# Splitting the next x within a step at the switch, and another order of stores and loads in the queue of a recurrent layer

## The chip, the cores and the metric

The kernel runs on one core of a Trainium2 chip. The metric is the time of the program on the device in microseconds (us), as the median of several runs. A profile comes from one further execution; its times are counted from the start of its span. The engines are named as the profile names them: PE (TensorE, the matrix unit; PEld are its weight loads), DVE (VectorE), ACT (ScalarE), POOL (GpSimd) and SP (SyncE, which issues nearly all DMA transfers of this kernel, in program order).

## The reference

x has 64 sequences of 256 steps with 1024 features, in float32. The first layer is a recurrence over the steps, added to its input:

```python
xW = jnp.einsum('ntd,dh->nth', x, Wx) + b
def step(prev_h, xw):
    next_h = jnp.tanh(prev_h @ Wh + xw)
    return (next_h, next_h)
x = x + h_of_all_steps
```

The second layer takes Haar differences and sums of its input over all levels, multiplies them by a gate of 1024 values per sequence (two small layers on the condition) and puts them together again. Since every part is multiplied by the same gate and the transform is undone, this is `v + v * gate`, and with the residual around it the result is `x * (2 + gate)`. The kernel calls `2 + gate` the `factor`.

## The kernel before, in words

All is computed in one pass over the steps t = 0 to 255. Two kinds of matrix products share PE.

*Products of h.* h (64 x 1024) times Wh is done by Strassen's seven products, in the order 1, 4, 2, 5, 6, 7, 3 (the calls of `strassen_product` in the loop over t, L1065 to L1104). Each is 32 small matmuls. `strassen_sides` forms the seven left sides from `hT`, the transposed h; side 4 is the quarter 3 of `hT` itself. The accumulators for the next step get their share of x @ Wx ahead of time by a copy on ACT (`put_part`, L632). Within a step DVE adds the products up (L1074, L1076, L1094, L1095, L1099, L1102, L1105), ACT takes the tanh (L1048) and DVE transposes the quarters (L1052). At the end of a step `residual` (L639 or L642) adds h to x on DVE.

*Products of x.* x of two steps (a "pair") is a 128 x 1024 tile. To reach float32 precision it is split in three: `x_high` by a mask (L138), `x2` by `difference` (L320), `x1` by `low` (L315) on DVE, and `x0` by `cast` (L326) on ACT. `beside_two` issues the products (L881): those with `x2` go to the banks `mixed`, those with `x1` and `x0` to the banks `main`. `both_mixed` takes the `mixed` banks out, and `finish(0)` and `finish(1)` (L802, on DVE) take the two `main` banks out. The products 5 and 7 of the next step of h write the same two banks. The finished sum of a pair goes to DRAM (`store_sum`, L789) and comes back in another layout as the shares of two steps: eight transfers (`reload_two`, L782), four for each step. POOL then adds the bias to each half (L785).

A *group* is one such set of products of x and the two steps of h that follow it. The last step of a group calls `beside_two` at its end, which issues the next group's work. From the 23rd step on (`SWITCH = 22`) a pair is one of three kinds. The first six are "plain". After that "one" and "two" alternate, 55 of each: the last two of the eight blocks of features of two pairs are done together by Strassen's method, for which weight forms are loaded again and again from DRAM (`load_slot`, L775), and in a "two" group POOL forms the sides for the following pair (L813 to L816), which DVE splits in the next step (L823, L826 and L831, by the lists `within` and `behind_residual`: what is in `within` runs in the first step of a group between the transpose of quarter 0 and L1094, what is in `behind_residual` after that step's `residual`).

*The switch.* Up to step 21 the results go out as pairs, from large tiles called slabs. From step 22 on each step's x is loaded by itself (`load_step`, L724, a tile `r` of 256 KB, three buffers), gets h added (L639), is multiplied by the factor on POOL (L861) and stored (`store_step`, L720). The slabs' space is given to new tiles at the end of step 21 (`start_of` is true in that call of `beside_two`), so that the first load of x after it waits for the last stores from slabs. In that call the x that is split is the pair 13.

*The order of the work.* It is written out by hand for all engines: each engine and SP's queue run their instructions in the order of the program. In `beside_two` a dictionary `at` says before which matmul of x the pieces of work on the other engines are placed, counted in matmuls; `per` is the number of matmuls to one bank. `not_ahead_of` makes `store_sum` wait for a copy in the last step of a group, so that transfers stay out of most of the products of h; what is behind it in SP's queue waits too.

Of the kernel before, what the change touches and what calls it, by code (L numbers as in the profile page):

```python
# [91 lines left out]
def tile_cond_resid(  # L92
# [193 lines left out]
    def bank(tag: str, name: str):  # L286
        return one_pool.tile([P, HALF], F32, tag=tag, name=name)
# [11 lines left out]
    class XWork:  # L299
# [12 lines left out]
        def low(self) -> None:  # L312
            i, x = self.i, pairs[self.i]
            self.x1 = split.tile([P, D], F32R, tag="x1", name=f"x1_{i}")
            nc.vector.tensor_sub(self.x1, x, self.high)  # L315

        def difference(self) -> None:
            i = self.i
            self.x2 = split.tile([P, D], F32R, tag="x2", name=f"x2_{i}")
            nc.vector.scalar_tensor_tensor(  # L320
                out=self.x2, in0=self.high, scalar=1.0 + DOWN, in1=pairs[i], op0=ALU.mult, op1=ALU.subtract
            )
# [63 lines left out]
        def finish(self) -> list:  # L386
            for h in range(2):
                self.finish_half(h)
            return self.relay()
# [84 lines left out]
    for k in range(B):  # L474
        x_block(k)
        split_block(k)
        if k == 0:
            now = XWork(1)
# [47 lines left out]
    for t in range(ALONE):  # L526
        i, s = divmod(t, S)
# [34 lines left out]
        if s == 1 and t + 1 < ALONE:  # L562
            now = later
# [62 lines left out]
    def quad(v, j: int):  # L626
        return v[:, j * E : (j + 1) * E]

    def put_part(t: int, j: int):

        part = bank(("acc", "m57", "gate")[j], f"acc{t}_{j}")[:, :E]
        nc.scalar.copy(part, xws[t // S][t % S][:, j])  # L632
        return part
# [78 lines left out]
    within, behind_residual, ready = [], [], {}  # L712
# [6 lines left out]
    def store_step(t: int) -> None:  # L719
        nc.sync.dma_start(out=yS[t - SWITCH], in_=steps.pop(t))  # L720

    def load_step(t: int):
        steps[t] = new["pool"].tile([P, W], F32, tag="r", bufs=3, name=f"r{t}")
        return nc.sync.dma_start(out=steps[t], in_=xS[t - SWITCH])  # L724
# [49 lines left out]
    def load_slot(p: int, j: int):  # L774
        return nc.sync.dma_start(out=weight(p, j).bitcast(F32), in_=forms_d[p][j])  # L775

    def reload_two(i: int, places: list, biased: bool) -> None:
        d = totals.pop(("d", i))[:].rearrange("(s g m) (q f) -> s q m g f", s=S, g=G, q=Q)
        xws[i] = places
        for s, v in enumerate(places):  # L780
            for q in range(Q):
                nc.sync.dma_start(out=v[q * R : (q + 1) * R].rearrange("m (g c) e -> m g (c e)", g=G), in_=d[s, q])  # L782
        for v in places if not biased else []:
            v = v[:].rearrange("p (g c) e -> p g (c e)", g=G)
            nc.gpsimd.tensor_add(v, v, new["b"][:].unsqueeze(1).broadcast_to((P, G, F)))  # L785
# [50 lines left out]

    def beside_two(t: int, now, mark):

        i = (t + 1) // S
        n = now.i  # L840
        start_of = t + 1 == SWITCH
        kind = "plain" if n < FIRST else "one" if n % 2 == 0 else "two"
        if start_of:
            totals[i] = later.sum
        store_sum(i, mark)
        places = [
            const.tile([P, 4, E], F32, tag="xw0", name=f"xw{t + 1}"),
            const.tile([P, 4, E], F32, tag="h0T", name=f"xw{t + 2}"),
        ]
        if start_of:  # L850
            reload_two(i, places, True)
# [14 lines left out]
        else:  # L866
            ends.append(new["pool"].tile([P, D], F32, tag="x", name="ends"))
            nc.sync.dma_start(out=ends[0][:, :W], in_=xN)
        load_step(t + 1)
        with_next = kind != "one" and n + 1 >= FIRST and n + 1 < NP  # L870
        if with_next:
            new["ahead"] = new["pool"].tile([P, 2 * P], F32, tag="ahead", name=f"ahead{n + 2}")
            nc.sync.dma_start(out=new["ahead"], in_=xT[n + 2][:, FULL * P :])
        if not start_of:
            reload_two(i, places, False)

        mixed, main = ([bank(f"{tag}{h}", f"{tag}{h}_{n}") for h in range(2)] for tag in ("mixed", "main"))
        x = (now.x0, now.x1, now.x2)
# [10 lines left out]
        nxt = [None]  # L889
# [25 lines left out]
        per = {"plain": B, "one": FULL + 1, "two": FULL}[kind]  # L915
# [58 lines left out]
        def finish(h: int) -> None:  # L974
            plus_main(left[:, cols(h)], main[h])

        at = {}
        if kind == "one":
            at = {
                7: [fifth],  # L980
                14: [mask],
                16: [first_two],
                25: [sixth],
                28: [low],
                34: [seventh],
                35: [lambda: finish(0), fourth_sum, third_sum],
            }
        else:
            at = {
                lead + 2 * per: [both_mixed, mask, difference],  # L990
                lead + 4 * per: [low],
                lead + 5 * per: [lambda: finish(0)],
            }
# [26 lines left out]
        while slots:  # L1020
            load_slot(*slots.pop(0))
        if not start_of:
            store_step(t - 1)
            store_step(t)
        load_step(t + 2)
        return nxt[0]

    jobs = [None]
# [4 lines left out]
    later, coming = beside_x(t, None, later, [t], None)  # L1033
    first = ALONE
    for t in range(ALONE, T):
        i, s = divmod(t, S)
        final = t == T - 1
        last_of_group = t == first + groups[0] - 1
        xw = xws[i][s]
        m16, m5, m7 = (bank(tag, f"{tag}_h{t}")[:, :E] for tag in ("m16", "main0", "main1"))  # L1040
        y = sums.tile([P, 4, E], F32, tag="y", name=f"y{t}")
        u = sums.tile([P, E], F32, tag="u", name=f"u{t}")
        h = work.tile([P, W], F32, tag="h", bufs=1, name=f"h{t}")
        hT = None if final else work.tile([P, W], F32, tag="hT", name=f"hT{t}")
        nxt = [None] * 3

        def tanh(j: int) -> None:
            nc.scalar.activation(quad(h, j), quad(h, j), AF.Tanh)  # L1048

        def transpose(j: int) -> None:  # L1050
            if not final:
                nc.vector.transpose(quad(hT, j), quad(h, j))  # L1052

        def put_next(j: int) -> None:
            if not last_of_group:
                nxt[j] = put_part(t + 1, j)

        def times_factor(v: slice) -> None:
            nc.vector.tensor_mul(h[:, v], h[:, v], ends[0][:, W + v.start : W + v.stop])

        def plus_x(v: slice) -> None:
            nc.vector.tensor_add(h[:, v], h[:, v], ends[0][:, v])
            nc.sync.dma_start(out=yT[i][:, W + v.start : W + v.stop], in_=h[:, v])

        strassen_product(m16, sides[1], 1, True)  # L1065
        nc.scalar.copy(y[:, 0], m16)
        if accs[1] is None:
            accs[1] = put_part(t, 1)
        if t == first and coming is not None:
            coming.cast()  # L1070
        strassen_product(accs[2], sides[4], 4)
        strassen_product(accs[0], sides[2], 2)
        strassen_product(m5, sides[5], 5, True)
        nc.vector.tensor_add(quad(h, 0), accs[0], y[:, 0])  # L1074
        tanh(0)
        nc.vector.tensor_add(y[:, 3], m5, xw[:, 3])  # L1076
        transpose(0)
        if final:
            times_factor(slice(0, E))
            plus_x(slice(0, E))  # L1080
        elif t > T - 4:

            v = steps[t - 1]
            nc.vector.tensor_mul(v, v, factor)
            store_step(t - 1)
        put_next(0)
        if t == first:
            while within:
                within.pop(0)()
        strassen_product(m16, sides[6], 6)  # L1090
        mark = nc.scalar.copy(u, m16)  # L1091
        if t >= SWITCH:
            loads_of(t, mark)
        nc.vector.tensor_add(y[:, 3], y[:, 3], u)  # L1094
        nc.vector.tensor_add(y[:, 2], accs[2], u)  # L1095
        put_next(2)
        strassen_product(m7, sides[7], 7, True)
        for o in (3, 2):
            nc.vector.tensor_add(quad(h, o), m7, y[:, o])  # L1099
        tanh(3)  # L1100
        tanh(2)
        nc.vector.tensor_add(y[:, 1], m5, u)  # L1102
        transpose(3)
        strassen_product(accs[1], sides[3], 3)  # L1104
        nc.vector.tensor_add(quad(h, 1), accs[1], y[:, 1])  # L1105
        tanh(1)
        if final:
            times_factor(slice(F, W))
            times_factor(slice(E, F))
            plus_x(slice(E, F))  # L1110
            plus_x(slice(F, W))
            break
        transpose(2)
        put_next(1)
        transpose(1)
        sides = strassen_sides(hT, t)
        accs = nxt
        if t == T - 2:
            residual(t, hT)
            nc.vector.tensor_mul(steps[t], steps[t], factor)  # L1120
            store_step(t)
        elif last_of_group:
            group = range(first, t + 1)
            first = t + 1
            del groups[0]
            if t + 1 < SWITCH:
                later, coming = beside_x(t, later, coming, list(group), mark)
            else:
                coming = beside_two(t, coming, mark)
        else:  # L1130
            residual(t, hT)
            while behind_residual:
                behind_residual.pop(0)()
# [38 lines left out]
```

## Time and profile before

| | |
|---|---|
| median of 3 runs | 3024.32 us (3021.7 to 3028.24) |
| the profiled execution | 3028.58 us |
| its span | 3026.7 us |
| PE busy in the span | 3007.1 us |
| DVE, POOL, ACT busy | 2204.1, 944.6, 915.9 us |
| mean granted clock of PE | 0.998 |
| transfers on SP's queue | 452.08 MB, 46.4% of the DMA engines' time |

A busy line gives an engine's time, its share of the span and its number of instructions. A line of waits reads: the engine and line that waited, the engine and line that ended the wait, the total in us, how many times, the longest. A line of the timeline gives start and duration in us, the engine, the line, the operation, its tiles and shapes, how many are merged, and in brackets the idle time before it with what ended it. A line of the window view gives the stretch, its length, the busy time of PE, PEld, DVE, ACT and POOL in it (instructions in parentheses), the clock granted to PE as a share of full speed, the busy share of the DMA engines and GB/s.

### The profile page before, as it was taken

Reading aid. Unit: us, or ns where it says so; the run is one execution under the profiler, and the core shown is the slowest. Engines: PE = TensorE matmul, PEld = TensorE weight load, DVE = VectorE, ACT = ScalarE, POOL = GpSimd, SP = SyncE. Lnnn points to the kernel's source line nnn. Section 1 sums busy time; section 2 is a strip of 40 time slices with the busy share of each in tenths; the row PEclk is TensorE's granted clock in tenths of the full one; section 3 lists DMA queues with packets and bytes.
Section 4 is the critical chain, followed back from the end, with each engine's and each line's share of the span. In section 5 each row is a group of like instructions: output and inputs, shape, how many; then the busy total and the mean of one; then the engine's idle time right before and its main releaser. Section 6 shows DMA issues by size and latency. Waiting matters only on the chain. (4 is left out here: it accounts for less than half of the span.)

```text
span 3026.7 us, 148299 instructions
## 1 busy us (share of the span) xinstructions
PE 3007.1 (99%) x63697; PEld 2680.0 (89%) x63697; DVE 2204.1 (73%) x5594; ACT 915.9 (30%) x2753; POOL 944.6 (31%) x800
## 2 busy tenths in 40 slices
PE   9999999999999999999999999999999999999998
PEld 6888888998898889988988988899889888898897
DVE  8555567777777777777777777777777777777776
ACT  3222222333333323223333332233332332332332
POOL 2233223332333332323323323333233333333322
PEclk9999999999999999999999999999999999999999
DMA  7334454445544544445445445444454454445543
GB/s 266 120 108 136 149 174 151 155 145 158 161 145 140 165 156 147 154 153 162 142 153 166 150 140 163 149 156 147 152 163 149 140 165 150 154 149 157 162 143 111
DMA packets 254196, 462.09 MB, mean 153 GB/s; under 512 B 35696, under 2 KB 109168, under 8 KB 253552
## 3 DMA queue, kind: packets, MB, share of 16 engines
q1 hardware_dynamic: 253408, 452.08, 46.4%
q8 instruction: 514, 8.42, 1.2%
q14 instruction: 130, 1.06, 0.1%
q10 hardware_dynamic: 144, 0.52, 0.1%
HBM read 313.00 MB, written 139.46 MB: 149 GB/s over the span
## 5 line engine op out<-in xcount | busy, mean ns | idle before, releaser
L881 PE MATMUL main<-wx,x 128*128 128x512 f32 x3052 | 746.4, 389 | 0.0
L861 POOL TENSOR_TENSOR r<-r,factor 128x512 f32<-128x512 f32 x230 | 317.9, 1382 | 1323.6 <-DVE r L639 1038.6
L881 PEld LDWEIGHTS main<-wx,x 128*128 128x128 f32 x3052 | 572.9, 188 | 119.1
L785 POOL TENSOR_TENSOR xw<-xw,b_h 128x512 f32<-128x512 f32 x230 | 363.2, 1591 | 345.9 <-DMA xw<-sum_d 318.5
L1048 ACT ACTIVATE h<-h 128x128 f32<-128x128 f32 x976 | 275.4, 306 | 524.7 <-DVE h L1074 314.3
L881 PE MATMUL mixed<-wx,x 128*128 128x512 f32 x1526 | 389.1, 399 | 0.0
L632 ACT COPY acc<-xw 128x128 f32<-128x128 f32 x726 | 186.1, 269 | 552.6 <-POOL xw L785 253.2
L881 PEld LDWEIGHTS mixed<-wx,x 128*128 128x128 f32 x1526 | 277.4, 188 | 76.6 <-issue 23.0
L1052 DVE STREAM_TRANSPOSE hT<-h 128x128 f32<-128x128 f32 x972 | 298.0, 307 | 39.9 <-ACT h L1048 38.2
L212 PE MATMUL acc<-wh,s 128*32 128x128 f32 x8160 | 273.6, 273 | 0.0
L212 PE MATMUL acc<-t,hT 128*32 128x128 f32 x8160 | 271.5, 273 | 1.1 <-DVE hT L1052 0.5
L212 PE MATMUL main_h<-t,s 128*32 128x128 f32 x7808 | 264.4, 273 | 7.8 <-DVE sum L802 5.8
L212 PE MATMUL acc<-wh,hT 128*32 128x128 f32 x8160 | 270.3, 273 | 0.0
L212 PE MATMUL m_h<-wh,hT 128*32 128x128 f32 x7808 | 262.0, 275 | 3.9 <-ACT u L1091 3.9
L212 PE MATMUL m_h<-t,s 128*32 128x128 f32 x7808 | 261.0, 273 | 0.0
L212 PE MATMUL main_h<-wh,s 128*32 128x128 f32 x7808 | 260.5, 273 | 0.0
L799 ACT ACTIVATE sum<-chain_mixed 128x512 f32<-128x512 f32 x220 | 131.6, 598 | 398.1 <-PE chain_mixed L881 398.1
L212 PEld LDWEIGHTS m_h<-wh,hT 128*32 128x32 f32 x7808 | 208.7, 110 | 46.9 <-issue 23.6
L212 PEld LDWEIGHTS acc<-wh,s 128*32 128x32 f32 x8160 | 231.2, 110 | 0.9 <-issue 0.9
L212 PEld LDWEIGHTS acc<-t,hT 128*32 128x32 f32 x8160 | 228.8, 110 | 2.8 <-issue 1.1
L212 PEld LDWEIGHTS main_h<-t,s 128*32 128x32 f32 x7808 | 221.4, 110 | 10.5 <-DVE sum L802 6.0
L212 PEld LDWEIGHTS acc<-wh,hT 128*32 128x32 f32 x8160 | 228.8, 110 | 0.1
(135 smaller groups left out, 4062.9 us busy)
## 6 DMA issues: line engine op xcount, KB each, us to landing
wx<-form SPq DMA_DIRECT2D x330, 256.0 KB, 3.0
x<-xT SPq DMA_DIRECT2D x128, 512.0 KB, 4.7
sum_d<-sum SPq DMA_DIRECT2D x127, 512.0 KB, 3.0
xw<-sum_d SPq DMA_DIRECT2D x1008, 64.0 KB, 3.2
r<-xS SPq DMA_DIRECT2D x233, 256.0 KB, 3.8
yS<-r SPq DMA_DIRECT2D x233, 256.0 KB, 4.1
ahead<-xT SPq DMA_DIRECT2D x55, 128.0 KB, 5.0
wh<-wh SPq DMA_DIRECT2D x8, 512.0 KB, 10.9
```

What stands on the lines that cost most here:

```text
L212: nc.tensor.matmul(out=out[q * R : (q + 1) * R], lhsT=a[:, k * R : (k + 1) * R], rhs=wh_s.sides[i][k][:, q], start=first and k == 0, stop= ...
L632: nc.scalar.copy(part, xws[t // S][t % S][:, j])
L785: nc.gpsimd.tensor_add(v, v, new["b"][:].unsqueeze(1).broadcast_to((P, G, F)))
L799: nc.scalar.activation(out, mixed, AF.Copy, scale=-1.0)
L861: nc.gpsimd.tensor_mul(steps[r], steps[r], factor)
L881: nc.tensor.matmul(out=out, lhsT=lhs, rhs=rhs, start=start, stop=stop, skip_group_check=True)
L1048: nc.scalar.activation(quad(h, j), quad(h, j), AF.Tanh)
L1052: nc.vector.transpose(quad(hT, j), quad(h, j))
```

## The change

It has two parts.

At the switch, mask, `difference`, `low` and `cast` of the next x are no longer placed beside the products of x in that call. `beside_two` returns the still empty list instead of the split x. Mask and `difference` are put into `within`, `low` and `cast` into `behind_residual`, so that they run in step 22. The next call takes the split x from the list.

In every call after that, and in part in that one, SP's queue has another order. The load of r for the first step of the next group moves from behind the load of x to the end, between the second y store and the other load of r. The first y store moves from behind the weight forms to the middle of the reloads of sums, behind the first four.

```diff
-    def reload_two(i: int, places: list, biased: bool) -> None:
+    def reload_two(i: int, places: list, biased: bool, between=None) -> None:
         for s, v in enumerate(places):
             for q in range(Q):
                 nc.sync.dma_start(out=v[q * R : (q + 1) * R].rearrange("m (g c) e -> m g (c e)", g=G), in_=d[s, q])
+            if s == 0 and between:
+                between()
...
     def beside_two(t: int, now, mark):
 
+        if isinstance(now, list):
+            now = now[0]
...
-        load_step(t + 1)
         with_next = kind != "one" and n + 1 >= FIRST and n + 1 < NP
...
         if not start_of:
-            reload_two(i, places, False)
+            reload_two(i, places, False, lambda: store_step(t - 1))
...
+        elif start_of:
+            at = {2 * per: [both_mixed], 5 * per: [lambda: finish(0)]}
         else:
             at = {
                 lead + 2 * per: [both_mixed, mask, difference],
...
         if not start_of:
-            store_step(t - 1)
             store_step(t)
+        load_step(t + 1)
         load_step(t + 2)
+        if start_of:
+            within.append(lambda: (mask(), difference()))
+            behind_residual.append(lambda: (low(), nxt[0].cast()))
+            return nxt
         return nxt[0]
...
-        if t == first and coming is not None:
+        if t == first and isinstance(coming, XWork):
             coming.cast()
```

## The prediction

> **What bounds the kernel now.** The page's first part says which engine fills the span:
>
> ```profile
> PE 3007.1 (99%) x63697; PEld 2680.0 (89%) x63697; DVE 2204.1 (73%) x5594; ACT 915.9 (30%) x2753; POOL 944.6 (31%) x800
> ```
>
> TensorE (PE) is busy for 3007.1 of 3026.7 us. Only what makes it wait can be won, so the waits of PE come next (us in total, times, longest):
>
> ```profile
> PE main_h L212 <- DVE sum L802: 5.8, 1, 5.8
> PE m_h L212 <- ACT u L1091: 3.9, 1, 3.9
> PE main_h L212 <- issue: 2.0, 4, 1.1
> ```
>
> The first is a single wait, for `finish` on VectorE. The second lies at 3002.9, in the last steps, which wait for the last reload. The window view gives the group of the first beside its neighbours:
>
> ```profile
> 275.08:298.55 23.47, 23.47 (x501) 21.11 (x497) 14.25 (x41) 6.92 (x23) 8.96 (x6) 1.00 0.45 138
> 298.55:329.94 31.39, 25.62 (x500) 22.68 (x496) 13.07 (x40) 6.79 (x22) 2.56 (x2) 0.89 0.38 139
> 329.94:353.41 23.47, 23.47 (x500) 21.10 (x496) 13.46 (x40) 6.76 (x22) 11.12 (x8) 1.00 0.37 116
> ```
>
> A group (x products, then two steps of h) takes 23.47 us with PE busy throughout; the group at the switch takes 31.39, so 7.92 us are lost there, the largest loss in the trace. The timeline of the switch tells why:
>
> ```profile
> 310.55 0.42 SPq L865 DMA_DIRECT2D x<-xT  x1
> 311.02 0.43 SPq L724 DMA_DIRECT2D r<-xS  x1
> ...
> 314.43 0.69 DVE L138 TENSOR_SCALAR x_high<-x 128x1024 int32<-128x1024 int32 x1 [13.26 <-DMA x<-xT]
> ...
> 315.23 1.23 DVE L320 SCALAR_TENSOR_TENSOR x<-x_high,x 128x1024 fp32r<-128x1024 f32 x1
> 316.37 1.22 DVE L315 TENSOR_TENSOR x<-x,x_high 128x1024 fp32r<-128x1024 f32 x1
> 317.50 1.28 DVE L802 SCALAR_TENSOR_TENSOR sum<-main,sum 128x512 f32<-128x512 f32 x2
> 318.24 1.94 PE L212 MATMUL main_h<-t,s 128*32 128x128 f32 x32 [5.77 <-DVE sum L802]
> ```
>
> VectorE sits 13.26 us at the mask (L138) for the next x, whose load SP could issue only at 310.55. The two `finish` (L802) are queued behind mask, difference and low. Product number 5 of step 22, the fourth in order, writes the bank that `finish(0)` reads, so PE waits from 312.47 to 318.24. Then PE runs at half clock for a while:
>
> ```profile
> 315.00:318.20 3.20, 0.00 (x0) 0.00 (x0) 3.10 (x5) 1.04 (x1) 0.00 (x0) 0.57 0.83 322
> 318.20:320.00 1.80, 1.76 (x36) 1.63 (x40) 0.78 (x2) 0.48 (x2) 0.00 (x0) 0.50 0.09 33
> 320.00:321.70 1.70, 1.70 (x40) 1.57 (x36) 0.51 (x2) 0.00 (x0) 0.00 (x0) 0.50 0.00 0
> 321.70:324.00 2.30, 2.30 (x80) 2.25 (x76) 1.39 (x6) 1.05 (x4) 0.00 (x0) 0.87 0.00 0
> ```
>
> So 5.77 us of the loss are the wait, and the other 2.15 mostly the slow clock after it (the blocks at 318.24 and 319.95 take 1.71 us start to start, against 0.87).
>
> **The change, part by part: the switch.** Mask, difference, low and cast leave the x window. `finish(0)` and `finish(1)` then wait for their products alone: as in the next group (339.41 and 341.23, with PE leaving the window at 341.05) they end at 308.7 and 310.5, before PE needs either bank (312.3). The wait of 5.77 and the slow clock go. What is late next: mask and difference now stand in step 22, between the transpose of quarter 0 and `y<-y,u` (L1094). I lay the next group's first step on the switch (its PE starts at 341.05, here 309.65: 31.40 earlier). The transpose would end at 313.98 and L1094 start at 345.99 - 31.40 = 314.59. The x load is issued as before, with nothing new ahead of it, so the mask starts at 314.43 again and L1094 at 316.37, the place that low has now: 1.78 late. Behind it on VectorE is the transpose of quarter 3, which step 23's second product in order (number 4, L1071) reads. In the pattern that transpose ends at 347.55 and the product starts at 348.06, a slack of 0.51. So PE stalls 1.78 - 0.51 = 1.27, say 1.3 us, at 316.66. The other transposes are 0.87 apart, like the products (0.87), and add nothing.
>
> Low and cast follow step 22's residual (about 319.6 to 320.3): low 1.2 us on VectorE, to 321.4, and cast 1.04 on ScalarE, about 318.4 to 319.5. Behind low waits step 23's first sum (L1074, due 319.95, so 1.5 late), behind cast the copy of m16, done by 319.8. What step 23's own products read was made in step 22; then come mixed products of x for 3.8 us, which need only the difference. They cover both; without that cover low's lateness would cost up to 1.5. The load of r for step 22 now stands behind top and low of Wx: low, issued at 311.97, takes 6.9 us to land (318.9), so r lands just before its use at 319.6; up to 3 us later would still be covered by the mixed products. POOL's order stays as it was.
>
> Bounds of the leftover stall: if x landed over 1.3 us sooner, 0; if it took the median of x loads, 4.7 us from issue instead of this one's 3.7, 2.3. I take 1.3, since the same load in the same queue was measured. Its clock: a stall of 1.07 us near 2999 kept 1.00:
>
> ```profile
> 2998.00:3000.00 2.00, 0.93 (x34) 0.66 (x23) 0.29 (x1) 0.31 (x1) 0.00 (x0) 1.00 0.05 16
> ```
>
> and the 5.77 us one lost it some 2.4 us in (0.57 as mean from 315.0), for about 6.8 us, that is 3.4 us of lost work if PE runs all along. 1.3 is nearest to 1.07, so I take 0 and keep 3.4 as the upper end. The Trainium skill, "TensorE: Matmul & The Clock Gate", Part 1, says that the clock halves after at least one idle window of about 3.4 us. By that rule no stall under 3.4 us costs clock and the sum is 3017.7 with no end above it; by the row, a drop after 2.4, it could be 3021.1, so the row decides.
>
> Switch: -7.92 + 1.3 = **-6.6 us**.
>
> **The queue, in 117 groups.** SP issues the same transfers: sum store, x, (ahead), four reloads, first y store, four reloads, (three forms), second y store, two r loads. The first r load moves back past 8 reloads, up to 3 forms and 2 stores: some 9 us later, issued near 1502.7 instead of 1493.4 in the group shown below, landing 3.8 later (median) at 1506.5; its reader (L639) runs at 1511.27, so 4.8 us of margin. After the other kind the margin is larger (issue 1523.6, reader at 1535.94). The first y store waits for a POOL product that ended at 1491.7, so it holds nothing up; it delays the second half of the reloads by its 0.43 us of issue. The second r load needed the first store landed:
>
> ```profile
> SPq L724 <- DMA yS<-r: 355.1, 116, 5.0
> ```
>
> This 3.1 us wait per group goes, but what is queued behind it is the next sum store, some 8 us later: 0. The first half of the reloads loses 256 KB ahead of it and lands up to 0.7 us sooner; the copies that need it (L632, 1502.72) are 0.6 ahead of PE (second product, 1503.82) already: 0. What is closest is the second half, in the 55 groups of kind "two":
>
> ```profile
> 1500.63 3.29 POOL L785 TENSOR_TENSOR xw<-xw,b_h 128x512 f32<-128x512 f32 x2 [2.72 <-DMA xw<-sum_d]
> ...
> 1505.25 0.46 POOL L816 TENSOR_TENSOR raw<-x,raw 128x128 f32<-128x128 f32 x1
> ...
> 1507.18 0.39 DVE L823 TENSOR_SCALAR s_high<-raw 128x512 int32<-128x512 int32 x1
> ...
> 1508.21 0.28 DVE L1094 TENSOR_TENSOR y<-y,u 128x128 f32<-128x128 f32 x1
> ```
>
> Both biases run without a gap, so the second half had landed before the first add ended; 0.43 later changes little, and even whole it fits in the 1.47 us from 1505.71 to 1507.18. I take 0. Bounds: small gaps between PE's blocks from 325 to 2990 (starts over the shortest of the same kind, 41 places) are 7.4 us in all. If all vanish, -7.4; if transfers now crowding the window's end double them, +7.4. The last reload has nothing put between, so the tail stays.
>
> **Sum.** The profiled execution took 3028.58 us, 1.9 around its span; it would take 3022.0. It stands 4.3 above the median of the runs, and the switch is in every run: 3024.32 - 6.6 = **3017.7 us** (0.22% less).
>
> **Rivals.** (1) The clock drops in the leftover stall, or x lands a microsecond later: 3.4 (or 1.0) back, 3021.1. For it: the windows run free of the program; against: 1.07 us did no harm. (2) The moved loads also thin out the small gaps; for it: after kind "one" the 256 KB at 1526.75 no longer fall on products of h. Half of 7.4 gone: 3014.0. (3) Slower: the store between the halves holds up the second bias, the sides and L823. Place: the 55 groups "two". It begins to cost when the second add slips 1.47 + 0.35 (slack of product 4 at 1509.93 behind the transpose that ends at 1509.58) = 1.82 us. Each 0.1 more costs 5.5 us; at 1.94 the gain is gone, at 2.05 it is slower by 0.2%, at 2.1 it gives 3017.7 + 15.4 = 3033. For it: a y store takes 4.1 us to land; against: 256 KB need 0.65 us at the 400 GB/s that the transfers near 306 reach.
>
> **How the numbers follow.** A measurement of this kernel can tell about 0.2%, 6.05 us, from no change. Forecast 55%, its own range 3015 to 3021; its gain is 5.6 to 7.9 by the bounds of the stall, so three quarters of it (41%) lie beyond 6.05. Rival 1 13%, rival 2 19%, rival 3 13%. Faster 41 + 19 = 60%; same 14 + 13 = 27%; slower 13%. The range takes in rivals 1 and 2 with a little for the runs' own spread (3021.7 to 3028.24) and leaves out rival 3 and the far end of 2: 3012.5 to 3024.5.
>
> **What would show it.** The switch group 24.8 us long, no PE wait for `finish`, a stall of 1.3 us before step 23's second product, clock 1.00 there; mask at 314.4 behind the transpose; SP without the wait of the r load for the y store; L823 not later against L1094. Wrong if PE waits more there, if the clock shows 0.5, or if the blocks after "two" windows spread.

## The result and the profile after

| | before | after |
|---|---|---|
| median of 6 runs each | 3025.48 us | 3038.16 us |
| lowest and highest | 3021.7 to 3028.66 | 3032.76 to 3042.25 |
| ratio after/before | | 1.0042, 95% interval 1.003 to 1.0054 |
| the profiled execution | 3028.58 us | 3032.76 us |
| its span | 3026.7 us | 3030.7 us |

The change makes the kernel 0.42% slower. The forecast was 3017.7 us, with 3024.5 as the upper end of its range.

The changed kernel has other line numbers: `finish` is L804 (was L802), the matmuls of x L884 (L881), the bias L787 (L785), the last side L818 (L816), its mask L825 (L823), the product with the factor L865 (L861), `y<-y,u` L1103 (L1094), `store_sum` L791 (L789). First the page's busy line of PE and its neighbours, for after:

```profile
PE 3014.4 (99%) x63697; PEld 2682.0 (88%) x63697; DVE 2214.8 (73%) x5594; ACT 916.2 (30%) x2753; POOL 938.5 (31%) x800
```

The instructions are the same in number on every engine; PE is "busy" for 7.3 us longer (3007.1 before). The waits of PE, after (us in total, times, longest):

```profile
PE acc L212 <- issue: 6.2, 16, 1.4
PE main_h L212 <- issue: 1.9, 4, 1.2
...
PE m_h L212 <- ACT u L1100: 0.4, 1, 0.4
```

The wait for `finish` is gone, as forecast. At the top there is now something that stood nowhere near it before: 16 waits in products of h that no semaphore ended ("issue"). The window view puts the times in their places. After: the switch group, the groups from there to the start of the last window of x products, and the tail.

```profile
298.82:324.16 25.34, 23.97 (x501) 21.29 (x497) 13.10 (x40) 6.60 (x22) 3.44 (x2) 1.00 0.49 174
324.16:2989.61 2665.45, 2659.73 (x56389) 2381.99 (x56389) 1987.63 (x5111) 814.90 (x2509) 838.86 (x735) 1.00 0.46 152
2989.61:3030.70 41.09, 34.89 (x939) 31.83 (x935) 25.20 (x83) 9.42 (x38) 6.42 (x5) 1.00 0.34 113
```

And before, the last two of these stretches (the switch group, 31.39 us, stands in the prediction):

```profile
329.94:2979.92 2649.98, 2648.70 (x56392) 2377.51 (x56388) 1976.02 (x5111) 814.40 (x2509) 846.01 (x735) 1.00 0.48 153
2979.92:3026.70 46.78, 36.70 (x939) 33.32 (x935) 26.35 (x83) 9.41 (x38) 6.39 (x5) 0.92 0.32 100
```

The difference of the spans is 0.3 (before the switch) - 6.05 (switch) + 15.47 (the groups) - 5.69 (tail) = +4.0 us. So the switch paid what it was to pay, and the same groups, with the same instructions, took 15.47 us longer. The tail is the same code in both; its wait for the last reload (3.9 us before, 0.4 after) is seen in some executions and not in others, as the table in the next section shows. Without the tail the two profiled executions differ by 9.7 us. The medians differ by 12.7; the profiled execution of after is the shortest of its six, that of before stands 3.1 us above the median.

*The switch, after* (timeline):

```profile
311.05 0.42 SPq L869 DMA_DIRECT2D x<-xT  x1
...
314.98 0.69 DVE L138 TENSOR_SCALAR x_high<-x 128x1024 int32<-128x1024 int32 x1 [0.73 <-DMA x<-xT]
...
315.71 1.23 DVE L320 SCALAR_TENSOR_TENSOR x<-x_high,x 128x1024 fp32r<-128x1024 f32 x1
...
316.86 0.28 DVE L1103 TENSOR_TENSOR y<-y,u 128x128 f32<-128x128 f32 x1
...
317.65 0.38 PE L212 MATMUL acc<-wh,s 128*32 128x128 f32 x2 [1.37 <-issue]
```

Mask and difference stand ahead of `y<-y,u`, as forecast, and PE loses 1.37 us once, at clock 1.00. But the loss is at the last two matmuls of step 22's seventh product, and no engine ended it.

*A "two" group, after* (timeline of SP; PE leaves the window of x products at 1503.63):

```profile
1498.17 0.37 SPq L720 DMA_DIRECT2D yS<-r  x1
1498.58 2.97 SPq L782 DMA_DIRECT2D xw<-sum_d  x4
1501.65 1.32 SPq L775 DMA_DIRECT2D wx<-form  x3
1503.06 0.38 SPq L720 DMA_DIRECT2D yS<-r  x1
1503.50 0.96 SPq L724 DMA_DIRECT2D r<-xS  x2
```

The same group before (the window ends at 1502.92):

```profile
1500.44 1.32 SPq L775 DMA_DIRECT2D wx<-form  x3
1501.85 0.86 SPq L720 DMA_DIRECT2D yS<-r  x2
1505.72 0.34 SPq L724 DMA_DIRECT2D r<-xS  x1
```

Before, the last load of r was issued 2.80 us behind the window's end, because it waited for the first y store to land. After, both loads follow at once. The waits of SP's queue no longer have a line for that landing; the wait has gone to the sum store of the next group (974.3 us before):

```profile
SPq L791 <- ACT u L1100: 1134.1, 116, 11.4
```

What the sides wait for has not become later. POOL and DVE, the same group after (two views, POOL first):

```profile
1501.10 3.54 POOL L787 TENSOR_TENSOR xw<-xw,b_h 128x512 f32<-128x512 f32 x2 [2.48 <-DMA xw<-sum_d]
...
1505.97 0.46 POOL L818 TENSOR_TENSOR raw<-x,raw 128x128 f32<-128x128 f32 x1
```

```profile
1507.89 0.38 DVE L825 TENSOR_SCALAR s_high<-raw 128x512 int32<-128x512 int32 x1
...
1508.91 0.28 DVE L1103 TENSOR_TENSOR y<-y,u 128x128 f32<-128x128 f32 x1
```

From the end of the last side (1506.43) to the mask are 1.46 us; over all "two" groups the median is 1.47 before and 1.47 after. The extra time is on PE itself. After, from 1508:

```profile
1508.89 1.05 PE L212 MATMUL acc<-wh,s 128*32 128x128 f32 x30
...
1510.60 0.38 PE L212 MATMUL acc<-wh,s 128*32 128x128 f32 x2 [0.66 <-issue]
...
1510.73 1.13 PE L212 MATMUL m_h<-wh,hT 128*32 128x128 f32 x32
```

Before, the same product runs through:

```profile
1508.18 1.06 PE L212 MATMUL acc<-wh,s 128*32 128x128 f32 x32
1509.06 1.06 PE L212 MATMUL m_h<-wh,hT 128*32 128x128 f32 x32
```

After 30 of 32 matmuls PE stops, as at the switch, and it goes on without a release. What it lacks, as the rest of this section shows, is its own instructions. The page's queues show that they come by DMA too (packets, MB, share of 16 engines):

```profile
q1 hardware_dynamic: 253408, 452.08, 44.9%
q8 instruction: 513, 8.40, 1.2%
```

513 packets of 16 KB hold 2 x 63697 matmuls and weight loads, about 248 in each. A product of h has 64 of them, so PE crosses from one packet to the next every four products or so. In this group the transfers of data (after, by the microsecond; last two columns are the busy share of the DMA engines and GB/s) run on until 1508:

```profile
1505.63:1506.63 1.00, 1.00 (x48) 1.00 (x42) 0.04 (x1) 0.61 (x1) 0.72 (x2) 1.00 1.03 393
1506.63:1507.63 1.00, 1.00 (x48) 1.00 (x40) 0.43 (x2) 0.49 (x2) 0.00 (x0) 1.00 0.84 322
1507.63:1508.63 1.00, 1.00 (x48) 1.00 (x40) 0.96 (x4) 0.27 (x1) 0.00 (x0) 1.00 0.13 43
```

The view of the queues shows only data from the window's end at 1503.63 to 1508.2 (packets, MB, share of the engines), after:

```profile
q1 hardware_dynamic: 751, 1.35, 82.7%
```

and the first packet of instructions in the stretch from 1508.2 to 1509.4, where the trace has its start at 1508.30, 4.67 us behind the window's end:

```profile
q8 instruction: 1, 0.02, 4.9%
```

Before, the transfers broke off earlier, and the packet started at 1505.69, 2.77 us behind the window's end; the two microseconds around it, before:

```profile
1504.92:1505.92 1.00, 1.00 (x48) 1.00 (x42) 0.04 (x1) 0.61 (x1) 0.71 (x2) 1.00 0.69 252
1505.92:1506.92 1.00, 1.00 (x48) 1.00 (x40) 0.43 (x2) 0.49 (x2) 0.00 (x0) 1.00 0.38 23
```

PE gets to the place in the seventh product 6.08 us behind the window's end (5.26 to the product's start, and 30/32 of 0.87). Here it went on 2.30 us behind the packet's start (1510.60 - 1508.30). So a packet that starts up to about 3.8 us behind the end costs nothing in this product, and one at 4.67 costs 0.9.

The same holds group by group. After, the packet starts over 3.7 us behind the window's end in 23 of the 55 "two" groups. In each of these 23 PE stops in the seventh product (by over 40 ns), in none of the other 32, and it goes on 2.2 to 2.4 us behind the packet's start. Before, there are 3 such groups, and PE stops in the same 3.

Over the 55 "two" groups, that first packet starts 2.87 us (median) behind the end before, and over 3.5 us in 4 of them; after it is 3.55 us, and 31 of them. The small gaps of PE from 325 to 2990 (starts over the shortest of the same kind, all of them) are 13.9 us before and 27.3 after. That is 13.4 of the 15.47 us. Those over 40 ns alone, the measure of the prediction, are 7.4 us at 41 places before and 20.9 at 78 after; 20.7 of the latter lie at two borders four products apart, 11.2 behind the seventh product of the first step and 9.5 behind the fourth of the second. Before, 5.7 of the 7.4 lay at the same two.

### The profile page after: what moved, and what is told of

Read it like the earlier page. It is cut to its first block, busy times and chain, and to the rows that moved or that the text cites. A ratio compares the mean times of both kernels' runs of the same rounds, so it can differ in the third digit from the quotient of the medians.

```text
span 3030.7 us, 148012 instructions
## 1 busy us (share of the span) xinstructions
PE 3014.4 (99%) x63697; PEld 2682.0 (88%) x63697; DVE 2214.8 (73%) x5594; ACT 916.2 (30%) x2753; POOL 938.5 (31%) x800
## 4 chain that ended last, share of the span: by engine, by line
PE 99%; DMA 0%; POOL 0%; issue 0%; DVE 0%; SPq 0%; ACT 0%; DVEq 0%; POOLq 0%
PE main L884 24%; PE acc L212 22%; PE m_h L212 15%; PE main_h L212 14%; PE mixed L884 13%; PE chain_main L884 3%; PE main L291 3%; PE chain_mixed L884 2%; PE mixed L291 1%; PE m L212 1%; PE acc L229 0%; PE gate_ps L229 0%; POOL sum L337 0%; DMA wx<-wx 0%; PE acc_raw L229 0%
## 5 line engine op out<-in xcount | busy, mean ns | idle before, releaser
L884 PE MATMUL main<-wx,x 128*128 128x512 f32 x3052 | 746.3, 389 | 0.0
L865 POOL TENSOR_TENSOR r<-r,factor 128x512 f32<-128x512 f32 x230 | 318.9, 1386 | 1345.8 <-DVE r L639 1060.1
L884 PEld LDWEIGHTS main<-wx,x 128*128 128x128 f32 x3052 | 572.8, 188 | 119.0
L787 POOL TENSOR_TENSOR xw<-xw,b_h 128x512 f32<-128x512 f32 x230 | 355.7, 1550 | 369.1 <-DMA xw<-sum_d 323.5
L884 PE MATMUL mixed<-wx,x 128*128 128x512 f32 x1526 | 389.4, 399 | 0.0
L884 PEld LDWEIGHTS mixed<-wx,x 128*128 128x128 f32 x1526 | 277.4, 188 | 76.8 <-issue 23.0
L212 PE MATMUL acc<-wh,s 128*32 128x128 f32 x8160 | 283.4, 273 | 6.0 <-issue 6.0
L212 PE MATMUL main_h<-t,s 128*32 128x128 f32 x7808 | 270.7, 273 | 2.3 <-issue 1.9
```

What stands on the lines that cost most here:

```text
L212: nc.tensor.matmul(out=out[q * R : (q + 1) * R], lhsT=a[:, k * R : (k + 1) * R], rhs=wh_s.sides[i][k][:, q], start=first and k == 0, stop= ...
L865: nc.gpsimd.tensor_mul(steps[r], steps[r], factor)
L884: nc.tensor.matmul(out=out, lhsT=lhs, rhs=rhs, start=start, stop=stop, skip_group_check=True)
```

## The experiments

Three theories stood at the start. A: the data transfers behind the "two" window come in one burst without SP's pause, and PE's packet of instructions comes late. B: the store between the reloads holds up the second bias, the sides and the mask. C: the first part of the change disturbs the later groups.

They were measured apart from the first pair, each beside runs of the kernel before on the same chip, so they are compared by the ratio to it. One table holds what the traces answer; "gaps" are those of all sizes as above, "packet" is the median start of the first packet behind the 55 windows, "late" those over 3.5 us, and "stops" the "two" groups in which PE stopped by over 40 ns in the product with the first border (the seventh, in the two shifted kernels the sixth).

| kernel | ratio, 95% | switch group | groups | tail | gaps | packet | late | stops |
|---|---|---|---|---|---|---|---|---|
| before | 1 | 31.4 | 2649.98 | 46.8 | 13.9 | 2.87 | 4 | 3 |
| after | 1.0042 (1.003 to 1.0054) | 25.3 | 2665.45 | 41.1 | 27.3 | 3.55 | 31 | 23 |
| switch_only | 0.998 (0.9971 to 0.9988) | 25.1 | 2643.30 | 41.2 | 9.6 | 2.78 | 0 | 0 |
| queue_only | 1.0072 (1.006 to 1.0085) | 31.4 | 2669.01 | 41.1 | 30.7 | 3.68 | 34 | 25 |
| store_between | 1.0011 (1.0002 to 1.0019) | 25.3 | 2650.51 | 46.4 | 14.0 | 3.27 | 17 | 6 |
| load_at_end | 0.9993 (0.9983 to 1.0002) | 24.7 | 2648.17 | 46.9 | 13.5 | 3.14 | 11 | 6 |
| more_ahead | 1.0006 (0.9997 to 1.0014) | 25.8 | 2648.22 | 44.3 | 11.9 | 3.07 | 8 | 4 |
| more_behind | 0.9984 (0.9976 to 0.9993) | 26.4 | 2645.82 | 41.1 | 11.5 | 2.81 | 3 | 2 |
| loads_held | 0.998 (0.9971 to 0.9989) | 25.1 | 2643.38 | 46.3 | 9.0 | 2.79 | 1 | 1 |
| loads_held_all | 0.9995 (0.9986 to 1.0003) | 24.6 | 2645.23 | 47.0 | 10.6 | 2.80 | 2 | 2 |
| after_shift | 1.0292 (1.0271 to 1.0313) | 29.5 | 2739.24 | 44.5 | 70.1 | 3.44 | 23 | 54 |
| switch_shift | 1.0149 (1.0134 to 1.0164) | 29.6 | 2690.58 | 44.8 | 47.6 | 2.53 | 7 | 21 |

The ratio comes from several executions, the other columns from the profiled one of each (for before the one shown above, which was not made beside the experiments).

### The two parts apart

**switch_only**: the first part of the change alone; SP's queue in its old order. Against the changed kernel:

```diff
+        load_step(t + 1)
         with_next = kind != "one" and n + 1 >= FIRST and n + 1 < NP
...
-            reload_two(i, places, False, lambda: store_step(t - 1))
+            reload_two(i, places, False)
...
         if not start_of:
+            store_step(t - 1)
             store_step(t)
-        load_step(t + 1)
         load_step(t + 2)
```

> Only the first part of the change: mask and difference, then low and cast, of the next x run in step 22; SP's queue is as before. Theory A (after the window of a group "two" the transfers now follow each other without a pause, and the load of PE's own instructions starts behind them, too late): the group at the switch falls from 31.4 to about 25.3 us, the gaps of PE with no releaser ("issue") stay as before (acc: under 1 us in all), so 6 us faster than before, 3019.5. Theory B (the store between the reloads delays the second bias on POOL and with it L823 on DVE): the same, since the store is at its old place. Theory C (the first part itself disturbs the later groups): as slow as the changed kernel, about 3038.

**queue_only**: the second part alone. Against the changed kernel:

```diff
...
-        elif start_of:
-            at = {2 * per: [both_mixed], 5 * per: [lambda: finish(0)]}
...
-        if start_of:
-            within.append(lambda: (mask(), difference()))
-            behind_residual.append(lambda: (low(), nxt[0].cast()))
-            return nxt
         return nxt[0]
...
```

> Only the second part: the first y store between the reloads, both r loads at the end; the switch as before. A and B: the stall of 5.8 us at the switch stays and the loss of the groups comes on top, 3038 + 6 = about 3044. C: as before, 3025.5.

Measured: 3011.59 us against 3016.64 for switch_only, and 3040.47 for queue_only. The first part gains 0.2%, the second loses 0.72%. C falls: with the first part alone the groups take 2643.30 us and not one packet is late. The groups, from one view each, switch_only and then queue_only:

```profile
323.79:2967.09 2643.30, 2643.07 (x56390) 2377.09 (x56389) 1971.49 (x5111) 814.21 (x2509) 834.00 (x735) 1.00 0.47 154
```

```profile
329.74:2998.75 2669.01, 2662.07 (x56392) 2383.43 (x56388) 1998.03 (x5111) 814.25 (x2509) 829.53 (x735) 1.00 0.45 152
```

The same matmuls, 25.71 us apart, and PE idle by 6.94 us instead of 0.23. And in queue_only both waits stand side by side, the switch's and the new one:

```profile
PE main_h L212 <- DVE sum L804: 5.5, 1, 5.5
PE acc L212 <- issue: 5.5, 15, 1.0
```

### The second part taken apart

**store_between**: the changed kernel with the first r load back at the front; the y store stays between the reloads.

```diff
+        load_step(t + 1)
         with_next = kind != "one" and n + 1 >= FIRST and n + 1 < NP
...
             store_step(t)
-        load_step(t + 1)
         load_step(t + 2)
```

> The changed kernel with the load of r for the first step back at the front of the queue; the first y store stays between the reloads. A: the last transfers of a group are forms 768 KB, store 256 KB and load 256 KB, as many bytes as forms and two stores of before, so the instructions are loaded at most 0.4 us later than before and the gaps stay near those of before: 3020 to 3025. B: all of the loss is here: about 3038, and L823 comes late against L1103.

**load_at_end**: the changed kernel with the first y store back at the end; the r loads stay together.

```diff
-            reload_two(i, places, False, lambda: store_step(t - 1))
+            reload_two(i, places, False)
...
         if not start_of:
+            store_step(t - 1)
             store_step(t)
```

> The changed kernel with the first y store back at the end; both r loads at the end. A: the burst behind the window is 768 + 512 + 256 KB, as long as in the changed kernel, and only then comes the wait of the last r load: most of the loss stays, 3032 to 3038. B: no loss, 3019.5, as with the first part alone.

Measured: 3022.62 and 3014.93 us, against 3016.64. Over switch_only these are 0.31% and 0.13%; the whole second part is 0.62% (1.0042 against 0.998). A had most of the loss at load_at_end, B all of it at store_between: neither has the split. What the table shows is a threshold: each half moves the packet by 0.36 to 0.49 us, to 3.14 and 3.27, which leaves most of them under the 3.7 us from which PE stops: 6 of 55 groups in each half. Both together move it by 0.77, to 3.55, and PE stops in 23. The ratios alone would not show it, since their intervals reach 0.1% to each side.

In store_between the last r load no longer waits for a landing (it is issued 0.26 us ahead of the window's end), so the pause is gone there, and 256 KB less stand in the burst. In load_at_end the last load still waits and is issued 2.82 us behind the end. So where the first y store stands behind the forms, the wait for its landing, and with it the pause, stays; A had overlooked that.

### Bytes, and the burst taken away

**more_ahead** and **more_behind**: switch_only with 256 KB more in each "two" group, a store of `factor` into scratch that nothing reads. In more_ahead it is issued ahead of the last r load, in more_behind behind it.

```diff
+        if with_next:
+            more = dram.tile([P, W], F32, tag="more", name=f"more{n}")
+            nc.sync.dma_start(out=more, in_=factor)
         load_step(t + 2)
```

> The first part alone (switch_only), and in the 55 groups "two" 256 KB more, a store of the unchanging factor to a scratch tile in DRAM, issued behind the second y store and ahead of the last r load. Nothing reads it and no order of the change is in it. Theory A (a longer burst behind the window makes the load of PE's instructions late): the first instruction packet after these windows starts at a median of about 3.4 us instead of 2.8, the small gaps of PE rise from 9.6 us to 20 or more, and the time stands 0.1 to 0.4% above before, against 0.2% below it for switch_only. Theory B (the store between the reloads holds up POOL, and DVE behind it): 0.2% below before, as switch_only.

```diff
         load_step(t + 2)
+        if with_next:
+            more = dram.tile([P, W], F32, tag="more", name=f"more{n}")
+            nc.sync.dma_start(out=more, in_=factor)
```

> The same 256 KB in the same groups, but issued behind the last r load, which waits for the landing of the first y store and so is issued some 2.9 us after the window, when the instruction packet is under way. A: the first packet stays at about 2.8 us and the extra transfer is over before the next packet at 6.7: within 3 us of switch_only, 0.1 to 0.3% below before. If the number of bytes alone mattered, and not their place: as slow as more_ahead.

Measured: 3020.27 and 3013.59 us, against 3017.92. The same bytes cost 0.26% ahead of the load and 0.04%, that is nothing that can be told, behind it. The groups show the sense of it (2648.22 against 2645.82; 8 late packets against 3), but only 2.4 us of the 6.7 between the medians; 3.2 us are the tail of the two profiled executions. A had expected a median packet at 3.4 us and 20 us of gaps or more for more_ahead; 3.07 and 11.9 came. So the pair speaks for A in direction and is weak in size.

**loads_held**: the changed kernel, but in "two" groups both loads of r wait for the first tanh of the next step. All data moves as in after, in the same order in the queue; the store stays between the reloads.

```diff
-        load_step(t + 1)
-        load_step(t + 2)
+        if with_next:
+            held.extend((t + 1, t + 2))
+        else:
+            load_step(t + 1)
+            load_step(t + 2)
...
-        tanh(0)
+        zeroth = tanh(0)
+        while held:
+            not_ahead_of(load_step(held.pop(0)), zeroth)
```

> The changed kernel, with its first y store between the reloads, but in the groups "two" both r loads wait for the first tanh of the next step, 3.3 us after the window, so that the pause is back. A: the first instruction packet starts by 2.9 us, the small gaps fall from 27.3 us to about 10, and the time is 0.1 to 0.3% below before. B: the second half of the reloads is as late as in the changed kernel, so 0.3 to 0.5% above before.

Measured: 3011.72 us against 3017.92, 0.998 with 0.9971 to 0.9989. SP in loads_held, in a "two" group:

```profile
1493.25 1.32 SPq L775 DMA_DIRECT2D wx<-form  x3
1494.66 0.39 SPq L720 DMA_DIRECT2D yS<-r  x1
1498.39 0.81 SPq L724 DMA_DIRECT2D r<-xS  x2
```

The pause of 3.34 us between store and loads is there again, and with it everything else. The groups of loads_held:

```profile
324.21:2967.59 2643.38, 2643.26 (x56390) 2377.29 (x56389) 2005.80 (x5111) 814.89 (x2509) 826.30 (x735) 1.00 0.46 154
```

2643.38 us against 2643.30 of switch_only, one late packet of 55. The whole loss of the second part is gone while its store still stands between the reloads, so B falls, and the moment of the two loads is what costs.

**loads_held_all**: the same in every group after the switch, not in the "two" groups alone (`if not start_of` for `if with_next`).

> The same with the r loads held in every group after the switch. A: the instruction packets after the other windows gain nothing more, since those were not late: as loads_held within 3 us; at best 0.3% below before. B: 0.3 to 0.5% above before.

Measured: 3017.39 us, 0.9995. It is 0.15% slower than loads_held, 5.67 us where 3 at most were expected. Its groups took 1.85 us longer; the rest isn't in its one profile beside that of loads_held, since both have the long tail (47.0 and 46.3). The profile of loads_held is the highest of its runs (3015.78, median 3011.72) and that of loads_held_all lies at its median (3017.68, 3017.39), so the long tail may be the rule in one and the exception in the other. That is argued, not shown.

### Only the places of PE's instructions

If packets are the cause, where their borders fall must matter, with every transfer of data as it was. The kernel already places its products against the blocks of 256 instructions (`addr_align`, ahead of the last products of a window). **after_shift** and **switch_shift** are the changed kernel and switch_only with that place 64 instructions, one product, off:

```diff
             if k == len(todo) - 2 or kind == "two" and k == len(todo) - 2 - EVEN:
-                nc.tensor.addr_align(BLOCK, PLACE - (3 * EVEN if k < len(todo) - 2 else 0))
+                nc.tensor.addr_align(BLOCK, PLACE + 64 - (3 * EVEN if k < len(todo) - 2 else 0))
```

> The changed kernel with the same instructions in the same order on every engine; only PE's instructions of the windows after the switch are placed 64 further in their blocks of 256 (L1003), that is, by one product of h. Theory A: the packets' borders lie one product (0.87 us) earlier in the steps, so that the packet after a window "two" is asked for 1.75 us after it instead of 2.62, but starts when the burst is over, at 3.5 as before, and is needed 0.87 us sooner: the gaps move from the end of the first step's seventh product to the end of its sixth, nearly all 55 groups have one, and the time rises by 20 to 45 us against the changed kernel, 1 to 2% above before. If the gaps came from any wait on another engine's work, the place of PE's instructions would change nothing: 0.4% above before.

> The same shift in the kernel with the first part alone, whose burst is over some 0.7 us sooner. A: the packet starts at about 2.8 us or sooner, 0.2 us too late for the new place at most: 0 to 10 us slower than switch_only, that is 0.2% below to 0.2% above before, and 20 us or more faster than after_shift. Otherwise as switch_only, 0.2% below before.

Measured: 3112.45 us (1.0292) and 3065.94 us (1.0149), against 3021.41. The stop moves with the border. PE in after_shift, a "two" group:

```profile
1549.56 1.05 PE L212 MATMUL main_h<-wh,s 128*32 128x128 f32 x31
...
1550.94 0.30 PE L212 MATMUL main_h<-wh,s 128*32 128x128 f32 x1 [0.33 <-issue]
...
1551.06 1.08 PE L212 MATMUL acc<-wh,s 128*32 128x128 f32 x32
```

It is now in the sixth product instead of the seventh. The sixth and the tenth product behind a "two" window take 1.65 and 1.19 us on the mean, where 0.87 is the usual and after had 1.07 and 1.02 in the seventh and the eleventh. The waits of PE in after_shift:

```profile
PE main_h L212 <- issue: 29.7, 42, 2.3
PE acc L212 <- issue: 19.2, 61, 1.1
```

The groups of after_shift take 73.8 us more than those of after (2739.24 - 2665.45). The ratio went up by 2.5%, where 20 to 45 us and 1 to 2% above before were expected. Not all of that is the new order: switch_shift, with the old order of the queue, loses 47.3 us to switch_only in its groups, where 0 to 10 were expected. So the new order costs 22.15 us with the old place (after over switch_only) and 48.66 with the new one (after_shift over switch_shift), more than twice as much when PE gets to its border one product sooner. The moment from which lateness costs moves with the border, too. In after the stops begin with packets that start 3.7 us behind the window; in both shifted kernels they begin with packets at about 2.8 us, one product (0.87 us) sooner. In after_shift that is 54 groups of 55, and PE goes on 2.2 to 2.6 us behind the packet's start there, much as in after. This is the sharpest evidence for A.

Of the 47.3 us of switch_shift 41.5 lie in the "two" groups: 9.8 in the sixth product, 7.8 in the tenth and 23.1 in the fourteenth, just ahead of the next window of x products. So the new place is worse with either order of SP's queue, and the old order is safe for one place of the border, not for any. Which transfers hold up the packet for the fourteenth product was not traced.

The gaps of the table do not hold all of the loss: they are 13.4 of 15.47 us between before and after, 17.7 of 22.15 between switch_only and after, 60.5 of 95.9 between switch_only and after_shift. They are counted over the shortest of the same kernel, which hides what every group of a kernel loses: the shortest fourteenth product takes 0.99 us in switch_only and 1.37 in after_shift. Counted from start to start of every product, the same traces hold the whole. Between before and after the "two" groups take 16.6 us longer (9.8 in the seventh product, 5.0 in the eleventh, 1.8 in the fourteenth) and all others 1.1 less. Between switch_only and after_shift it is 87.2 us (41.6 in the sixth, 17.1 in the tenth, 28.5 in the fourteenth) and 8.7 in the others.

## Why the prediction was wrong

*The switch: right.* The group was to last 24.8 us and lasted 25.34 (24.58 to 25.35 in the five other runs that carry the change there with the old places of PE's instructions and no bytes added). The gain is 6.05 us for 6.6, the wait for `finish` is gone, the mask starts at 314.98 (314.4), the clock stays at 1.00. The 1.3 us of leftover stall came out as 1.37, but by luck: it was to be a wait for DVE's transpose ahead of step 23's second product, and it was PE's lack of instructions in step 22's seventh, where the packet started at 315.44 and PE went on at 317.65. The delay on DVE was there as forecast: laid, as in the prediction, on the next group's first step of before, the transpose of quarter 3 ended 1.76 us late (1.78 forecast), which with the slack of 0.51 is some 1.25 us of stall by the prediction's own sum. The stop for instructions, just ahead, covered it. In load_at_end, where that stop was 0.37 us, a part of the forecast wait came through:

```profile
317.69 1.08 PE L212 MATMUL acc<-t,hT 128*32 128x128 f32 x32 [0.32 <-DVE hT L1062]
```

switch_only shows what the part is worth: 5.05 us between the medians, 0.2%.

*The clock.* The 1.37 us stop kept 1.00 in the switch group, as the 1.07 us one did before, so rival 1 fell. The prediction misread the row of the long wait: the granted clock of before is 1.00 up to 315.45 and 0.50 from 315.50, so it fell 3.0 us into the 5.77 us, not 2.4. In the tail of before it fell 2.3 us into the wait of 3.9 us (PE idle from 3002.89, clock 1.00 up to 3005.15 and 0.50 from 3005.20). The Trainium skill, "TensorE: Matmul & The Clock Gate", Part 1, has the clock drop only after at least one idle window of some 3.4 us. That the stops of 1.07 and 1.37 us cost no clock agrees with it; the drops after 3.0 and 2.3 us come sooner than it says, and the measurement decides.

*The queue: wrong, and this is the step that failed.* "This 3.1 us wait per group goes, but what is queued behind it is the next sum store, some 8 us later: 0." The step looked for instructions behind the waiting one on SP's queue, and there it was right. It left out that while SP waited nothing was added to the transfers on their way. In the group shown they ran out near 1505.7, and another queue, that of PE's instructions, got its packet through there (1505.69). queue_only gives the price in place of that 0: 0.72%, or 21.7 us on 3016.64 (3016.64 x 0.0072); loads_held puts a pause back and the price is gone (0.998, as switch_only).

*The moved load and the store between: right as far as they went.* The r load's reader did not wait; the sides had their 1.47 us before and after. Low and cast, moved behind the residual, made nothing wait. Rival 3 had the sign and the groups, but another mechanism: its store held nothing up. Rival 2 had the small gaps, with the sign the wrong way round.

*The bounds.* The one place that named the right thing was the bound "if transfers now crowding the window's end double them, +7.4". By the same measure the gaps grew by 13.5 us (7.4 to 20.9), so it was about half of what was needed: it took twice the present gaps for an end. Nothing made it stop there. The stops begin when the packet starts 3.7 to 3.8 us behind the window, and the median packet of before stood 0.9 us below that. With all 55 packets as late as the one shown, 0.9 us at each of two borders, the estimate of the end would have been near 100 us. With the old place of the borders no run lost that much; queue_only lost most, 25.71 us over switch_only.

*The tail.* It was to stay. In the profiled executions it went from 46.78 to 41.09, but kernels with the same tail code have both: 41.1 in queue_only, 46.9 in load_at_end. The long tail before also lost clock (0.92 on the mean against 1.00). It is put down to the execution, not to the change; what decides it is open.

The clue was in the profile of before: a queue called "instruction", small gaps of PE of which 5.7 of 7.4 us lay at two borders of products, and a kernel that aligns its products to blocks of 256 instructions. The prediction summed the gaps and did not ask what they were.

## What to carry to other kernels

A wait in a DMA queue that nothing behind it minds can still be useful: it is a pause in which other queues get through, and the one to ask for first is the queue that brings the bound engine its instructions. Where an engine is 99% busy and stops with no releaser in the same place of a loop, look up when its next packet of instructions started and which transfers ran until then. Take the good part of such a change alone (here switch_only), or give the moved transfers a moment of their own (loads_held): both are 0.2% faster than before, and 0.6% faster than the whole change.

## What the runs showed of the hardware that was not expected

- PE's instructions come in packets of 16 KB (8.40 MB in 513). In the group shown, where transfers of data held the DMA engines at 322 to 393 GB/s, the next packet started at 4.67 us behind the window instead of 2.77. PE, 99% busy, then stood with no releaser, here for 0.66 us, at the switch for 1.37. The Trainium skill, "Runtime: NRT & Kernel Launch", Instruction fetch mechanics, says of the same 16 KiB blocks that the next is fetched during the current one and that crossing a border is mostly hidden. The size agrees with the trace; the hiding holds at the first border behind the "two" windows in switch_only (PE stops in 0 of 55 groups) and does not in after (23 of 55) or after_shift (54).
- Where the border falls in the stream is worth up to 2.5% with no other difference: 1.0292 for after_shift against 1.0042, and 1.0149 for switch_shift against 0.998.
- Lateness of a packet costs nothing up to a point, and that point is set by the border: 3.7 us behind the window with the old place, about 2.8 us with the border one product (0.87 us) sooner.
- The last steps take 41.1 or 44.3 to 47.0 us in executions whose code there is the same, with 0.4 to 0.8 or 3.1 to 4.0 us of wait for the last reload.
